# Four graph layers on one core: the first layer's sums on column quarters, TensorE in a written order, and smaller moves at the ends of layers

## The chip, the core and the metric

One core of a Trainium2 chip runs the whole program. The core has TensorE (PE, matrix products into PSUM), VectorE (DVE), ScalarE (ACT), GpSimd (POOL) and SyncE (SP, which issues DMAs here). The metric is the device time of one execution in microseconds (us); the median of several runs is compared.

## The reference, cut to what matters

`x` is 4096 x 256, `adj` 4096 x 4096 (0 or 1). Four attention layers follow each other, each with a residual and a layer norm:

```python
x = _layernorm(x + L0(x, adj, W, a))       # additive attention, 4 heads of 64
x = _layernorm(x + L1(x, adj, Wq, .., bv)) # multi-head attention, 4 heads of 64
x = _layernorm(x + L2(x, adj, W, a))       # additive attention, 1 head
x = _layernorm(x + L3(x, adj, Wq, Wk))     # cosine attention
# L0: e = leaky_relu(s_i[i,h] + s_j[j,h], 0.2), -inf where adj == 0
#     alpha = softmax over j; out = elu(sum_j alpha[i,j,h] * Wh[j,h,:])
# L1: softmax(q k / 8 + (adj.T - 1) * 10000) @ v
# L2: as L0 with one head and slope 0.01
# L3: 0.5 * (softmax(where(adj > 0, Kn @ Qn.T, NEG)) @ x) + 0.5 * x
```

## The kernel before, in words

All matrices are fp32. `X` stays in SBUF: 32 tiles of 128 nodes (`NT`), in 8 blocks of 512 nodes (`NB`, `QB` = 4 tiles a block), with one more column of ones, which gives the softmax denominators in the last layer. Each layer goes over the 8 blocks b of destination nodes, and in each over source tiles j: 32 of 128 rows in layers 0, 2 and 3, and 64 of 64 rows in layer 1. `weights(b, j)` makes the masked, unnormalised attention `prob` of one unit; `sums(b, j)` multiplies it with the values into accumulators in PSUM; when a block is through, outputs are divided, joined with `X` and layer-normed under the next block.

Layer 0 (`additive_heads`): `weights` is four ACT operations (L256, one a head, on a broadcast `row` of the destination's terms) and one DVE multiplication with the mask (L257). `prob` has 8 buffers, `mask` 5 (two units each, loaded by SP). `sums` (L266, L270) runs over a group of four units at a time: first for all units four products with 64 columns of values a head, in column halves of the array, then four with one column of denominators, broadcast to 32 columns, in quarters. `acc` has three PSUM banks, in two buffers, and `ga_ps` two further banks. `prepare(b)` makes the values of four tiles: PE transposes of X (L110), ACT or DVE copies of them (`xT`, L111), products with W (L169), three small ACT exponentials a tile (L171 to L173), and a DVE multiplication into V (L174). `rows(b)` transposes the destination terms (L239), and sends them through DRAM to get `row` on all partitions. `outputs` transposes `kept`, a copy of the finished `acc` (L281), divides, applies elu, and adds to X.

The order on all engines in this layer comes from the framework's scheduler, which follows its own costs and may move one helper's instructions between another's; each engine then runs its list strictly in that order.

Layer 1 (`multi_head_attention`) begins with a prologue: `keys(b)` transposes a block of X, copies it by ACT, and makes keys and queries (L457); `values(b)` makes V (L471). A bound on the scores (`shift`) comes from the largest keys and queries (L490 to L500). The tail of layer 0 (its block 7) stands behind `keys(0)`. In the main part the order of PE, DVE and ACT is written out by hand, three units of lag between `weights` (L526 PE, L528 ACT, L531 DVE) and `sums` (L552). Score tiles `p` have three buffers, which the small PE jobs of `finish` use in turn with them. The row sums of `prob` are collected in three places of `den`: even units by GpSimd (L538), odd units by accumulating DMAs from GpSimd's queue (L544), in two places by turns. `join_sums` (L560) adds these on DVE at j = 7 and 9 of the next block; then follow the row sums on PE (L568), their copy, transpose and reciprocals, and the output in two `half` steps (L584, L587, L592).

Layer 2 (`additive_one`) prepares blocks 0 and 1, then runs layer 1's tail for block 7, then its units. Layer 3 (`cosine_attention`) makes scores (L723), exponentials (L726), masks (L727) and sums (L733), and at a block's end divides, adds 1.5 X, normalises and stores (L744 to L749); the last block in two stores.

Of the kernel before, what the change touches and what calls it, by code (L numbers as in the profile page):

```python
# [9 lines left out]
FP = mybir.dt.float32  # L10
# [4 lines left out]
OP = mybir.AluOpType  # L15
# [3 lines left out]
P = 128  # L19
# [9 lines left out]
def kernel(  # L29
# [47 lines left out]

    X = feat.tile([P, NT, D + 1], FP, name="X")
    nc.vector.memset(X[:, :, D:], 1.0)
# [81 lines left out]
    def additive_values(sb, bank, b, w_sb, V, src, dst, H, slope, busy=False):  # L161

        g = 1.0 - slope
        xT = transposed_block(sb, bank, b, (nc.scalar.copy if busy else nc.vector.tensor_copy, nc.scalar.copy))
        for k in range(QB):
            t = b * QB + k
            pw = bank()
            for c in range(KC):
                nc.tensor.matmul(pw[:, :D + 2 * H], xT[:, c, k * P:(k + 1) * P], w_sb[:, c, :],  # L169
                                 start=(c == 0), stop=(c == KC - 1))  # L170
            nc.scalar.activation(src[:, t, :], pw[:, D:D + H], AF.Exp, scale=g)  # L171
            nc.scalar.activation(dst[:, t, :], pw[:, D + H:D + 2 * H], AF.Exp, scale=g)
            nc.scalar.activation(V[:, t, D:], pw[:, D + H:D + 2 * H], AF.Exp, scale=slope)  # L173
            nc.vector.tensor_tensor(V[:, t, :D].rearrange("p (h d) -> p h d", h=H),  # L174
                                    pw[:, :D].rearrange("p (h d) -> p h d", h=H),
                                    V[:, t, D:].unsqueeze(2).to_broadcast([P, H, D // H]), OP.mult)

    def take(po, rden, H):

        o = fin.tile([P, D], FP, name="o")  # L180
        heads = "p (h d) -> p h d"
        nc.vector.tensor_tensor(o.rearrange(heads, h=H), po.rearrange(heads, h=H),
                                rden.unsqueeze(2).to_broadcast([P, H, D // H]), OP.mult)
        return o
# [11 lines left out]
    def additive_heads(a, H, slope, early, narrow):  # L196
# [7 lines left out]
        with ExitStack() as lay:  # L204
# [13 lines left out]
            mp = pool(lay, "ga_mask", 5)  # L218
# [9 lines left out]
            def first_rows():  # L228
                row[0] = rp.tile([P, H, QW], FP, name="row")
                for h in range(H):  # L230
                    pr = bank()
# [4 lines left out]
            def rows(b):  # L236

                pr = bank()
# [21 lines left out]
            def sums(b, js):  # L260
                if js[0] == 0:
                    acc[b] = pa.tile([P, HC + 1, QW], FP, name="acc")
                for j in js:
                    for h in range(H):
                        lo = (h % 2) * d
                        nc.tensor.matmul(acc[b][lo:lo + d, h // 2, :], V[:, j, h * d:(h + 1) * d], prob[b, j][:, h, :],  # L266
                                         start=(j == 0), stop=(j == NT - 1))
                for j in js:
                    for h in range(H):
                        nc.tensor.matmul(acc[b][h * G:(h + 1) * G, HC, :], V[:, j, D + h:D + h + 1].to_broadcast([P, G]),  # L270
                                         prob[b, j][:, h, :], start=(j == 0), stop=(j == NT - 1))
                if js[-1] == NT - 1:
# [5 lines left out]
            def outputs(bank, b, k):  # L278
                po = bank().rearrange("p (c f) -> p c f", f=P)
                for c in range(HC + 1):  # L280
                    nc.tensor.transpose(po[:, c, :], kept[b][:, c, k * P:(k + 1) * P], ident)  # L281
                rden = fin.tile([P, H], FP, name="rden")
                nc.vector.reciprocal(rden, po[:, HC, ::G])
                add_elu(take(po[:, :HC, :].rearrange("p c f -> p (c f)"), rden, H), b, k, mvs[b])
                if k == QB - 1:
                    layernorm_block(b, mvs[b])
# [571 lines left out]
```

## Time and profile before

| | |
|---|---|
| median of 3 runs | 3020.97 us (3019.48 to 3023.22) |
| profiled execution | 3020.11 us, its span 3018.3 us |
| layer 0, sums | 19.8 to 755.6 us |
| layer 1, prologue | 755.6 to 857.6 us |
| layer 1, main part | 857.6 to about 1793 us |
| layers 2 and 3 | to 3018.3 us |
| PE busy | 2960.5 us |
| granted PE clock | 0.996 of full |

The page of the profile lists busy time by engine; a table by stretches of time gives the same for chosen windows. A timeline line has start, duration, engine, line of the code, operation, tiles, count, and in brackets the idle time ahead of it with what ended it. A line of the waits has the waiting engine, line and tile, what it waited for, and then total us, times, and the longest. Products of fp32 count as two instructions each.

### The profile page before, as it was taken

The page shows a single profiled execution, that of the slowest core. Times are in us where ns is not written, and L with a number is a line of the kernel's source. Part 1 is how long each engine was busy: PE and PEld are TensorE (multiplying, and loading weights), DVE is VectorE, ACT ScalarE, POOL GpSimd, SP SyncE. Part 2 cuts the span into 40 slices and gives each one's busy share as a digit, 9 for nine tenths or more (in the row PEclk, how much of TensorE's full clock was granted, in tenths as well). Part 3 has the DMA queues.
Part 4 walks back from the last instruction along what each step waited for, and adds up shares of the span by engine and source line. Part 5 has one row for each costly group of instructions (what it writes and reads, how often), then busy time and mean ns, then how long its engine had stood idle before and what let it go on. Part 6 is the DMA issues. An engine that isn't in the chain of part 4 may idle for free.

```text
span 3018.3 us, 46664 instructions
## 1 busy us (share of the span) xinstructions
PE 2960.5 (98%) x18557; PEld 1568.0 (52%) x18557; DVE 1972.3 (65%) x2537; ACT 1672.8 (55%) x2653; POOL 862.4 (29%) x598
## 2 busy tenths in 40 slices
PE   9999999999999999999999989999999999999998
PEld 4333333333543333333333338888887777777776
DVE  7799999998457877878778764555655333333333
ACT  6799999997356556566566554444444322222222
POOL 0000000000058888889888860000000000000000
PEclk9999999999999999999999999999999999999999
DMA  7466767665048889889888872444442333333321
GB/s 196 84 134 136 138 133 139 134 121 93 1 108 192 173 179 192 171 183 185 175 183 183 176 173 88 142 154 152 153 140 61 51 56 57 63 50 62 63 49 21
DMA packets 204941, 373.05 MB, mean 124 GB/s; under 512 B 13249, under 2 KB 89009, under 8 KB 203826
## 3 DMA queue, kind: packets, MB, share of 16 engines
q0 software_dynamic: 101120, 176.18, 36.5%
q1 hardware_dynamic: 103328, 193.62, 20.2%
q8 instruction: 145, 2.38, 0.3%
q14 instruction: 74, 0.61, 0.1%
q10 hardware_dynamic: 274, 0.26, 0.0%
HBM read 315.43 MB, written 21.03 MB: 111 GB/s over the span
## 4 chain that ended last, share of the span: by engine, by line
PE 93%; DVE 3%; ACT 2%; issue 1%; DMA 1%; POOL 0%; DVEq 0%; ACTq 0%; POOLq 0%
PE acc L266 15%; PE acc L733 15%; PE p L526 13%; PE acc L552 13%; PE acc L270 8%; PE acc L370 7%; PE g L370 7%; PE p L723 4%; PE g L723 3%; PE g L169 2%; PE g L457 2%; DVE prob L531 1%; ACT p L528 1%; PE g L471 1%; PE acc L684 1%
## 5 line engine op out<-in xcount | busy, mean ns | idle before, releaser
L531 DVE TENSOR_TENSOR prob<-p,mask 128x1024 f32<-128x1024 f32 x512 | 620.4, 1221 | 211.5 <-ACT p L528 200.3
L528 ACT ACTIVATE p<-p,shift 128x1024 f32<-128x1024 f32 x512 | 555.6, 1088 | 347.3 <-PE p L526 337.2
L256 ACT ACTIVATE prob<-row,dst 128x512 f32<-128x512 f32 x1024 | 642.0, 710 | 41.1 <-PE acc L270 38.4
L538 POOL TENSOR_TENSOR den<-den,prob 128x1024 f32<-128x1024 f32 x248 | 615.2, 2481 | 82.1 <-DVE prob L531 72.2
L257 DVE SCALAR_TENSOR_TENSOR prob<-prob,mask 128x2048 f32<-128x2048 f32 x256 | 584.0, 2288 | 45.3 <-ACT prob L256 38.9
L526 PE MATMUL p<-qT,kT 64*64 64x512 f32 x4096 | 531.8, 591 | 10.3 <-DVE prob L531 9.5
L552 PE MATMUL acc<-prob,V 64*64 64x512 f32 x4096 | 531.2, 590 | 8.6 <-DVE prob L531 4.4
L733 PE MATMUL acc<-X,prob 128*128 128x257 f32 x2048 | 486.4, 380 | 2.7 <-DVE prob L727 2.7
L733 PEld LDWEIGHTS acc<-X,prob 128*128 128x128 f32 x2048 | 387.4, 190 | 167.4 <-issue 118.4
L266 PE MATMUL acc<-prob,V 128*64 128x512 f32 x2048 | 461.6, 596 | 0.2 <-DVE prob L257 0.2
L727 DVE TENSOR_TENSOR prob<-prob,mask 128x512 f32<-128x512 f32 x256 | 176.8, 691 | 414.0 <-ACT prob L726 409.5
L721 POOL DMA_DIRECT2D mask<-in_adjT x32 | 28.1, 881 | 1123.2 <-DVE prob L727 562.4
L362 ACT ACTIVATE e<-row,dst 128x512 f32<-128x512 f32 x256 | 184.2, 721 | 239.2 <-DVE prob L364 209.4
L552 PEld LDWEIGHTS acc<-prob,V 64*64 64x64 f32 x4096 | 155.9, 133 | 294.1 <-issue 278.1
L526 PEld LDWEIGHTS p<-qT,kT 64*64 64x64 f32 x4096 | 153.0, 133 | 289.9 <-issue 256.5
L364 DVE SCALAR_TENSOR_TENSOR prob<-e,mask 128x512 f32<-128x512 f32 x256 | 176.3, 689 | 179.5 <-PE acc L370 97.3
L266 PEld LDWEIGHTS acc<-prob,V 128*64 128x64 f32 x2048 | 141.1, 137 | 283.1 <-issue 236.2
L270 PE MATMUL acc<-prob,V 128*32 128x512 f32 x2048 | 237.1, 595 | 0.0
L544 POOL DMA_DIRECT2D den<-prob x240 | 223.0, 929 | 45.0 <-DVE prob L531 39.6
L726 ACT ACTIVATE prob<-p 128x512 f32<-128x512 f32 x144 | 86.0, 597 | 260.2 <-PE p L723 246.2
L370 PE MATMUL g<-V,prob 128*128 128x257 f32 x1024 | 226.5, 380 | 0.0
L370 PE MATMUL acc<-V,prob 128*128 128x257 f32 x1024 | 225.0, 380 | 0.0
(139 smaller groups left out, 2069.8 us busy)
## 6 DMA issues: line engine op xcount, KB each, us to landing
den<-prob POOLq DMA_DIRECT2D x240, 512.0 KB, 5.2
mask<-in_adjT SPq DMA_DIRECT2D x128, 512.0 KB
mask<-in_adjT SPq DMA_DIRECT2D x64, 1024.0 KB
mask<-edges SPq DMA_DIRECT2D x256, 128.0 KB
mask<-in_adjT POOLq DMA_DIRECT2D x32, 1024.0 KB, 8.3
edges<-in_adj POOLq DMA_DIRECT2D x32, 512.0 KB, 9.6
den<-prob SPq DMA_DIRECT2D x16, 512.0 KB
row<-far SPq DMA_DIRECT2D x7, 1024.0 KB
```

Of the source, the lines that this page charges most:

```text
L256: nc.scalar.activation(z[:, h, :], row[b][:, h, :], AF.Relu, bias=-1.0, scale=dst[:, j, h:h + 1])
L257: nc.vector.scalar_tensor_tensor(z, z, 1.0, mask[m][:, j % MJ, :].unsqueeze(1).to_broadcast([P, H, QW]), OP.add, OP.mult)
L266: nc.tensor.matmul(acc[b][lo:lo + d, h // 2, :], V[:, j, h * d:(h + 1) * d], prob[b, j][:, h, :], start=(j == 0), stop=(j == NT - 1))
L270: nc.tensor.matmul(acc[b][h * G:(h + 1) * G, HC, :], V[:, j, D + h:D + h + 1].to_broadcast([P, G]), prob[b, j][:, h, :], start=(j == 0), s ...
L370: nc.tensor.matmul(acc[b][k][:, :D + 1], prob[b, j][:, k * P:(k + 1) * P], V[:, j, :], start=(j == 0), stop=(j == NT - 1))
L526: nc.tensor.matmul(p[c * d:(c + 1) * d, r, :], kT[half, c, j * d:(j + 1) * d], qT[half, c, cols], start=True, stop=True)
L528: nc.scalar.activation(p, p, AF.Exp, bias=shift)
L531: nc.vector.tensor_tensor(z, p, mask[m][:, j % MJ, :].unsqueeze(1).to_broadcast([P, KC, QW]), OP.mult)
L538: nc.gpsimd.tensor_tensor(to, to, flat, OP.add)
L544: nc.gpsimd.dma_start(to, flat, accum_op=OP.add)
L552: nc.tensor.matmul(acc[b][r * d:(r + 1) * d, c, :], V[half, j, r * d:(r + 1) * d], prob[b, j][half, r, :], start=(j == 0), stop=(j == NH - 1))
L733: nc.tensor.matmul(acc[b][k], prob[b, j][:, k * P:(k + 1) * P], X[:, j, :], start=(j == 0), stop=(j == NT - 1))
```

## The change

In layer 0 each unit's sums are twelve products on 32 columns: two for the value columns of each head and one for its denominators; outputs are rearranged to fit. Each unit is summed by itself, two units behind its weights. PE's order there and in the prologue of layer 1 is the order of the program. `prepare` has three tiles in one three-bank accumulator (`side`) and the fourth in a bank, with one set of exponentials and one multiplication for the three. The transposes (`turn`) stand one block ahead of the products. Outputs of a block are transposed two at a time, with the steps of the layer norm at stated units, and the row transpose of the block after next at j = 4. The transposes of block 0 for layer 1 are in the last block of layer 0 (`ahead`). In the prologue of layer 1, `values` of the block before stands between a block's transposes and its keys, and the bound on the scores (`greatest`) between the last two `values`. In the main part the row sums, reciprocals and halves of the block before are at j = 12, 14, 17 and 19 (before: 10, 12, 15 and 18). The two joins of the last block are on GpSimd. In layer 3 the column of X holds twos, 1.5 X is made by ACT eight units ahead of a block's end, and the last two units of the last block are summed accumulator by accumulator. The cut below leaves out removed lines of the first layer's loop, which are in the listing above.

```diff
-    nc.vector.memset(X[:, :, D:], 1.0)
+    nc.vector.memset(X[:, :, D:], 2.0)
...
+    def additive_values(xT, b, groups, w_sb, V, src, dst, H, slope):
         g = 1.0 - slope
-        xT = transposed_block(sb, bank, b, (nc.scalar.copy if busy else nc.vector.tensor_copy, nc.scalar.copy))
-        for k in range(QB):
-            t = b * QB + k
-            pw = bank()
-            for c in range(KC):
-                nc.tensor.matmul(pw[:, :D + 2 * H], xT[:, c, k * P:(k + 1) * P], w_sb[:, c, :],
-                                 start=(c == 0), stop=(c == KC - 1))
-            nc.scalar.activation(src[:, t, :], pw[:, D:D + H], AF.Exp, scale=g)
-            nc.scalar.activation(dst[:, t, :], pw[:, D + H:D + 2 * H], AF.Exp, scale=g)
-            nc.scalar.activation(V[:, t, D:], pw[:, D + H:D + 2 * H], AF.Exp, scale=slope)
-            nc.vector.tensor_tensor(V[:, t, :D].rearrange("p (h d) -> p h d", h=H),
-                                    pw[:, :D].rearrange("p (h d) -> p h d", h=H),
-                                    V[:, t, D:].unsqueeze(2).to_broadcast([P, H, D // H]), OP.mult)
-    def take(po, rden, H):
-        o = fin.tile([P, D], FP, name="o")
-        heads = "p (h d) -> p h d"
-        nc.vector.tensor_tensor(o.rearrange(heads, h=H), po.rearrange(heads, h=H),
-                                rden.unsqueeze(2).to_broadcast([P, H, D // H]), OP.mult)
-        return o
+        heads = "p k (h d) -> p k h d"
+        for k, n, pw in groups:
+            for i in range(n):
+                for c in range(KC):
+                    nc.tensor.matmul(pw[:, i, :D + 2 * H], xT[:, c, (k + i) * P:(k + i + 1) * P], w_sb[:, c, :],
+                                     start=(c == 0), stop=(c == KC - 1))
+            t = slice(b * QB + k, b * QB + k + n)
+            s, d = pw[:, :, D:D + H], pw[:, :, D + H:D + 2 * H]
+            nc.scalar.activation(src[:, t, :], s, AF.Exp, scale=g)
+            nc.scalar.activation(dst[:, t, :], d, AF.Exp, scale=g)
+            nc.scalar.activation(V[:, t, D:], d, AF.Exp, scale=slope)
+            nc.vector.tensor_tensor(V[:, t, :D].rearrange(heads, h=H), pw[:, :, :D].rearrange(heads, h=H),
+                                    V[:, t, D:].unsqueeze(3).to_broadcast([P, n, H, D // H]), OP.mult)
...
-            mp = pool(lay, "ga_mask", 5)
+            mp = pool(lay, "ga_mask", 4)
...
-            def sums(b, js):
-                if js[0] == 0:
+            def sums(b, j):
+                if j == 0:
                     acc[b] = pa.tile([P, HC + 1, QW], FP, name="acc")
-                for j in js:
+                for n in range(HC + 1):
                     for h in range(H):
-                        lo = (h % 2) * d
-                        nc.tensor.matmul(acc[b][lo:lo + d, h // 2, :], V[:, j, h * d:(h + 1) * d], prob[b, j][:, h, :],
+                        lo = h * d + n * G
+                        part = V[:, j, lo:lo + G] if n < HC else V[:, j, D + h:D + h + 1].to_broadcast([P, G])
+                        nc.tensor.matmul(acc[b][h * G:(h + 1) * G, n, :], part, prob[b, j][:, h, :],
                                          start=(j == 0), stop=(j == NT - 1))
-                for j in js:
-                    for h in range(H):
-                        nc.tensor.matmul(acc[b][h * G:(h + 1) * G, HC, :], V[:, j, D + h:D + h + 1].to_broadcast([P, G]),
-                                         prob[b, j][:, h, :], start=(j == 0), stop=(j == NT - 1))
-                if js[-1] == NT - 1:
+                if j == NT - 1:
...
...
+            def turned(bank, b, k):
                 po = bank().rearrange("p (c f) -> p c f", f=P)
                 for c in range(HC + 1):
                     nc.tensor.transpose(po[:, c, :], kept[b][:, c, k * P:(k + 1) * P], ident)
+                return po
+            def outputs(po, b, k):
                 rden = fin.tile([P, H], FP, name="rden")
                 nc.vector.reciprocal(rden, po[:, HC, ::G])
+                o = fin.tile([P, D], FP, name="o")
+                nc.vector.tensor_tensor(o.rearrange("p (h c e) -> p h c e", h=H, c=HC),
+                                        po[:, :HC, :].rearrange("p c (h e) -> p h c e", h=H),
+                                        rden.unsqueeze(2).unsqueeze(3).to_broadcast([P, H, HC, G]), OP.mult)
+                add_elu(o, b, k, mvs[b])
+            def finish(b, j):
+                if j in (4, 10):
+                    k = (j - 4) // 3
+                    pos[b, k], pos[b, k + 1] = turned(bank, b, k), turned(bank, b, k + 1)
+                    if k == 0 and b + 2 < NB:
+                        rows(b + 2, pos[b, 0][:, HC + 1, :])
+                if j in (4, 7, 10, 13):
+                    k = (j - 4) // 3
+                    outputs(pos[b, k], b, k)
+                elif j == 15:
+                    roots[b] = begin_root(mvs[b])
+                elif j == 18:
+                    end_root(*roots[b])
+                elif j in (19, 21, 23, 25):
+                    k = (j - 19) // 2
+                    scale_row(X[:, b * QB + k, :D], mvs[b], roots[b][1], k)
+            def turn(b):
                 if b + 2 < NB:
                     load_x(b + 2)
+                busy = (nc.scalar.copy if b == 0 else nc.vector.tensor_copy, nc.scalar.copy)
+                xTs[b] = transposed_block(sb, bank, b, busy)
+            def prepare(b):
+                groups = [(0, HC + 1, side), (HC + 1, 1, bank().rearrange("p (n f) -> p n f", n=1))]
+                additive_values(xTs[b], b, groups, w_sb, V, src, dst, H, slope)
+            pos, roots, xTs = {}, {}, {}
+            LAG = 2
+            units = [(b, j) for b in range(NB) for j in range(NT)]
+            with tc.manual_schedule(engines={mybir.EngineType.PE}):
+                side = pa.tile([P, HC + 1, QW], FP, name="acc")
+                nc.tensor.matmul(side[:, 0, :], ones[:1, :], a_row, start=True, stop=True)
+                attach(keep, w_sb, side[:, 0, :], H)
+                turn(0)
+                prepare(0)
+                first_rows()
+                turn(1)
+                for i in range(len(units) + LAG):
+                    if i < len(units):
+                        b, j = units[i]
                         weights(b, j)
+                        if (b, j) == (1, 4 * QB):
+                            early()
+                        if i % 8 == 4:
+                            narrow(prob[b, j])
+                    if i >= LAG:
+                        b, j = units[i - LAG]
+                        sums(b, j)
+                        if b:
+                            finish(b - 1, j)
+                    if i == 0 or i % QB == 3 and 3 + i // QB <= NB:
+                        b = 1 if i == 0 else 2 + i // QB
+                        if b + 1 < NB:
+                            turn(b + 1)
+                        prepare(b)
+                        if b == 3:
+                            rows(1, bank())
+                    if i == (NB - 1) * NT + 20:
+                        ahead(bank)
...
+                def turn(b):
+                    xTs[b] = transposed_block(sb, bank, b, (nc.scalar.copy, nc.scalar.copy))
...
-                keys(0)
-                tail(bank)
-                values(0)
-                for b in range(1, NB - 1):
-                    keys(b)
-                    if b < NB - 2:
-                        values(b)
-                keys(NB - 1)
...
+                with tc.manual_schedule(engines={mybir.EngineType.PE}):
+                    keys(0)
+                    tail(bank)
+                    for b in range(1, NB):
+                        turn(b)
+                        if b < NB - 1:
+                            values(b - 1)
+                        keys(b)
+                    values(NB - 2)
+                    greatest()
+                    values(NB - 1)
...
-            def join_sums(b, n):
-                nc.vector.tensor_tensor(den[b][:, 0, :], den[b][:, 0, :], den[b][:, n, :], OP.add)
+            def join_sums(b, n, eng=nc.vector):
+                eng.tensor_tensor(den[b][:, 0, :], den[b][:, 0, :], den[b][:, n, :], OP.add)
...
-                elif j == 10:
+                elif j == 12:
                     row_sums(halves(), b)
-                elif j == 12:
+                elif j == 14:
                     reciprocals(halves(), b)
-                elif j in (15, 18):
-                    half(halves(), b, (j - 15) // 3 * 2)
+                elif j in (17, 19):
+                    half(halves(), b, j - 17)
...
-            join_sums(b, 1)
-            join_sums(b, 2)
+            join_sums(b, 1, nc.gpsimd)
+            join_sums(b, 2, nc.gpsimd)
...
-            def sums(b, j):
-                if j == 0:
+            def sums(b, js):
+                if js[0] == 0:
                     acc[b] = [pa.tile([P, D + 1], FP, name=f"acc{k}") for k in range(QB)]
                 for k in range(QB):
-                    nc.tensor.matmul(acc[b][k], prob[b, j][:, k * P:(k + 1) * P], X[:, j, :],
-                                     start=(j == 0), stop=(j == NT - 1))
+                    for j in js:
+                        nc.tensor.matmul(acc[b][k], prob[b, j][:, k * P:(k + 1) * P], X[:, j, :],
+                                         start=(j == 0), stop=(j == NT - 1))
...
-                        nc.vector.tensor_scalar(y[:, k, :], acc[b][k][:, :D], rden, 0.5, OP.mult, OP.mult)
-                        nc.vector.scalar_tensor_tensor(y[:, k, :], X[:, t, :D], 1.5, y[:, k, :], OP.mult, OP.add)
-                        one_row(mv, k - k0, y[:, k, :])
-                    normalise([y[:, k, :] for k in range(k0, k0 + n)], mv)
-                    nc.sync.dma_start(ov[:, b * QB + k0:b * QB + k0 + n, :], y[:, k0:k0 + n, :])
+                        nc.vector.scalar_tensor_tensor(y[b][:, k, :], acc[b][k][:, :D], rden, y[b][:, k, :], OP.mult, OP.add)
+                        one_row(mv, k - k0, y[b][:, k, :])
...
-                    sums(b, j)
+                    if j == NT - 8:
+                        y[b] = in_.tile([P, QB, D], FP, name="y")
+                        nc.scalar.mul(y[b], X[:, b * QB:(b + 1) * QB, :D], 1.5)
+                    if i < len(units):
+                        sums(b, [j])
+                    elif i > len(units):
+                        sums(b, [j - 1, j])
...
+        def ahead(bank):
+            bm_sb["x"] = transposed_block(wp, bank, 0)
```

## The prediction, made before the change was run

> **What bounds the kernel now.** I read the page first, then the table by stretches of time, TensorE's timeline and the list of waits stage by stage, and last the chain of waits near its end. The page's first line of busy time:
>
> ```profile
> PE 2960.5 (98%) x18557; PEld 1568.0 (52%) x18557; DVE 1972.3 (65%) x2537; ACT 1672.8 (55%) x2653; POOL 862.4 (29%) x598
> ```
>
> TensorE (PE) is busy 98% of 3018.3 us and carries 93% of the chain. Only two things shorten the run: PE doing the same work in less time, and the 58 us in which PE stands still. A busy PE is not PE at its peak, so the timeline of the first layer must say what a matmul costs. One 512-column fp32 product is two instructions. Inside a run, weight loads follow each other every 0.43 us, so an instruction slot is 0.429 us, shared by two products on 64-column tiles and by four on 32-column tiles.
>
> ```profile
> 289.97 7.09 PE L266 MATMUL acc<-prob,V 128*64 128x512 f32 x32
> 296.99 3.64 PE L270 MATMUL acc<-prob,V 128*32 128x512 f32 x32
> 300.56 7.09 PE L266 MATMUL acc<-prob,V 128*64 128x512 f32 x32
> ```
>
> See the starts: 7.02 us for 32 instructions in halves (16 slots = 6.86, so 0.16 over), 3.57 for 32 in quarters (8 slots = 3.43, 0.14 over). About 0.15 us is lost whenever the tile shape changes. In block 0 it is worse, because other work cuts these runs:
>
> ```profile
> 34.47 0.60 PE L110 MATMUL g<-ident,X 128*128 128x128 f32 x4
> 35.00 1.07 PE L266 MATMUL acc<-prob,V 128*64 128x512 f32 x2
> 36.01 1.90 PE L270 MATMUL acc<-prob,V 128*32 128x512 f32 x10
> 37.84 0.66 PE L110 MATMUL g<-ident,X 128*128 128x128 f32 x4
> ```
>
> Here one head alone (x2) takes 1.01 us, although two heads could share those slots. How near the other engines are, from the table by stretches over one later block (us busy):
>
> ```profile
> 256.30:343.12 86.82, 86.82 (x529) 26.48 (x525) 82.28 (x70) 81.77 (x138) 3.85 (x8) 1.00 0.66 134
> ```
>
> The columns are PE, weight loads, VectorE (DVE), ScalarE (ACT), GpSimd. PE has no gap; DVE needs 82.3 and ACT 81.8 of 86.8. That is the floor under any gain of PE here. PE's waits in the first layer sum to some 6 us, most of it at the start. Its waits in the layer-1 prologue, in the main part of layer 1, and at the change to layer 2 are:
>
> ```profile
> PE g L457 <- ACT xT L111: 3.4, 8, 1.5
> PE g L496 <- DVE qtop L491: 1.9, 1, 1.9
> ...
> PE p L526 <- DVE prob L531: 9.5, 15, 1.1
> PE p L568 <- DVE den L560: 8.2, 7, 1.2
> PE acc L552 <- DVE kept L557: 4.3, 7, 0.9
> ...
> PE acc L552 <- DVE prob L531: 4.4, 1, 4.4
> PE g L110 <- DVE kept L557: 4.4, 1, 4.4
> ```
>
> **What the Trainium skill says.** "TensorEngine Tiling (Array Packing)", Key Properties: changing the tiling mode drains the array, and tiles run independently. The trace agrees with both: 0.14 to 0.16 us a change, four 32-column products in one slot. "TensorE: Matmul & The Clock Gate", Architectural detail: ACT and DVE are strict FIFO, and PE only pulls weight loads ahead. The trace shows the FIFO at 1788.83 us, where a join that waits 3.76 us for a DMA holds back a product mask. "SBUF — State Buffer", SBUF: two separate sides: a DVE operation with two SBUF inputs and a GpSimd operation exclude each other. The trace agrees: L592 takes 0.68 us alone and up to 2.44 under a GpSimd addition.
>
> **The change, part by part.**
>
> *First layer, blocks 1 to 7 (148.1 to 755.63, 607.5 us).* A unit is now 12 products on 32 columns instead of 4 on 64 and 4 on 32: 24 instructions, 6 slots, 2.573 us, and no change of shape. Before it was 10.59/4 = 2.647. A block's sums are 32 x 2.573 = 82.3. The output transposes now come in two groups of six: 6 x 0.11 us each (the step from L281 x3, 0.48, to x12, 1.47), 0.15 into and 0.15 out of their shape, plus 0.1 for the row transpose, together 2.0. A block is 84.4 against 86.8, and seven save about 17 us. Transposing block 0 for layer 1 moves into the last block: +1.2. Net 15.5. ACT at 81.8 and DVE at 82.3 fit, with 2 us to spare; eight `prob` buffers give about five units (13 us) of lead, which covers the stretch of j 4 to 25 where DVE has the outputs (22 x 2.2 plus some 11, against 58.6 of PE). SP's `mask` ring goes from 5 tiles to 4: eight units or 20 us ahead is still far over a landing of 10 us, and no wait for `mask` is on the list in this layer; I cost it at 0. The row DMAs are queued about four units later, and masks behind them on SP: 0, at worst 2 us a block. Range of the part: 5 to 17.
>
> *First layer, block 0 (19.8 to 148.1, 128.3 us).* The trace has 97.9 us of sums there (64.7 L266 + 33.2 L270), against 82.3 uncut, and 34.6 of L169 and L110. New, in a fixed order: 82.3, then 96 L169 instructions x 0.223 = 21.4, 40 transposes x 0.11 = 4.4, and 13 changes of shape, 2: 110. The start should be alike: initial values, `first_rows` and two turns put the first sum near 20.5. ACT saves six small activations a group (0.17 each, partly pipelined), and DVE's two multiplications on V cost about 1.4 instead of 4 x 0.42: both hidden, since 4 units need 10.0 + 1.6 of ACT and 8.8 + 2.1 of DVE under 15.4 of PE. New wait: the fourth value group takes the bank of the first transposes, so PE waits for DVE's copy of `xT`. PE has 3.4 us of own work before it, and the copy needs 0.7 plus at most one or two 2.2 us products ahead of it in DVE's FIFO: 0 to 2 us six times, I take 0.5. Behind that wait on PE stand the next sums, then ACT and DVE through the `prob` buffers. Block ends near 133.5: 14.5 us gained, range 7 to 17.
>
> *Layer 1, prologue (755.63 to 857.64).* Block 0's transposes (1.05) and the 1.51 wait behind them leave; five or six waits of 0.24 to 0.29 for `xT` are hidden by `values` of the block before (3.65 us of PE against a copy of 0.6); block 7 keeps its 0.38. The 1.9 us wait for `qtop` goes under `values` of block 6. Sum 5.5, range 2 to 6.5. The 0.8 us wait for V at its end stays.
>
> *Layer 1, main part.* Row sums come two units (3.4 us) later, which removes the 1.17 us wait seven times: 8.2. But the two output halves move from 3 units apart to 2. Each gives DVE 0.68 + 2.44 (locked out by L538) beside 2.4 of products in 3.44 us of PE. Following the three `p` buffers by hand, I get about 1.3 us of PE waits a block, where the trace has 0.48: +0.9 x 7 = 6. Net 2 gained. Not shown before in this spacing, so from 8 gained to 6 lost.
>
> *Change to layer 2.* Two joins of 1.22 us on DVE, which waited 3.76 and 5.56 us for accumulating DMAs, go to GpSimd at 2.48 each (L538). DVE is then free for the last product mask, `kept` and `xT`: both 4.4 us waits of PE go. The new chain is last mask at about 1786.8, DMA out at 1787.6 and landed by 1793.6, or by 1797 if the first join is issued ahead of it, second join done between 1796 and 1800. Its user, the row sums L568, stands behind two preparations of PE, near 1802. Hidden by 2 to 6 us. Half a microsecond may come back from `kept` and `xT` copies meeting. 8.2 gained, range 3 to 9.
>
> *Last layer.* `y` = 1.5 X on ACT (about 1.1 us, under ACT's 2 us of idle time a unit) and the row of twos take one 0.48 us operation out of four in the final DVE chain: 4 x 0.4. The last two units are summed k by k, so the first accumulator is done 1.5 us earlier (4 instructions after the last-but-two unit, in place of 10). The chain from 3007.22 to the last scaling at 3014.15 then ends some 2.8 us earlier, range 1.5 to 3.5. Earlier blocks' outputs have no PE wait: 0.
>
> **Sum.** 15.5 + 14.5 + 5.5 + 2 + 8.2 + 2.8 = 48.5 us. The profiled execution took 3020.11 (span 3018.3 and 1.8 around it), 0.9 below the median of 3020.97: 3020.11 - 48.5 = 2971.6, about 2972. All best ends: 2960; all worst, 18 gained: 3003.
>
> **Rivals.**
> (a) *ACT and DVE become the bound in layer 0.* For: 82 us of 84.4, and PE's fixed order turns each late prob into a wait of PE. Against: five units of lead. If blocks run at 86 us, 11 of the gain go, and with 0.5 us more per preparation and 4 lost in layer 1 it ends near 2990.
> (b) *Slower: quarters don't keep the slot.* If the value products, with three accumulator banks in turn and a fresh weight tile for every product, took a longer slot than L270, 256 units x 6 slots multiply it: 0.03 us a slot is 47 us and eats everything, 0.1 makes it 3077. Against it: L270 already runs on quarters with the same four moving operands at 0.446 us a slot with its change of shape, and its loads of 0.11 us are hidden.
> (c) *The fixed order undoes the whole.* A stall of PE for `xT`, rows or `mask` of 6 us a block in layer 0 gives 48 us back: no change. Against it: everything awaited is issued four units or more ahead.
>
> **Chances.** Forecast as worked out (2960 to 2982) 0.66; (a) 0.23; (b) 0.05; (c) 0.06, half of it past zero. 0.2% of 3021 is 6 us, about what a measurement of this kernel can tell from no change. Faster 0.90, within 0.03, slower 0.07. The range of 8 in 10 is 2960 to 2991: the forecast and most of (a).
>
> **What would show it.** Right: one row of 128*32 sums with starts 2.57 us apart; blocks of 84 to 85 us; layer 0 ending near 727; L568 with no wait; the joins on GpSimd and the first transposes of layer 2 within 2 us of the last L552. Wrong: quarter runs above 0.44 us a slot; PE idle for DVE or ACT in layer 0 over 10 us; waits of L526 up by more than 8 us.

## The result and the profile after

The changed kernel takes 2971.24 us in the median against 3022.09 before: a ratio of 0.983, 95% interval 0.9813 to 0.9848. The forecast was 2972. The profiled execution has a span of 2969.5 us against 3018.3, 48.8 us less. The four runs of the changed kernel lie between 2966.5 us, with a mean granted clock of 0.999, and 2974.6 with 0.997. Each stage below is read from one profiled execution of either kernel, between starts that both timelines show:

| stage, us | before | after | gained | forecast |
|---|---|---|---|---|
| start to the first sum | 19.8 | 24.9 | -5.1 | -0.7 |
| layer 0, block 0 | 128.3 | 110.2 | 18.1 | 15.2 |
| layer 0, blocks 1 to 7 | 607.5 | 591.8 | 15.7 | 15.5 |
| layer 1, prologue, to the first score product | 102.0 | 94.7 | 7.3 | 5.5 |
| layer 1, main part, to the last score product | 925.6 | 921.9 | 3.8 | 2 |
| change to layer 2, to its first run of x18 (L370, now L400) | 40.7 | 33.3 | 7.4 | 8.2 |
| on to the last sums of layer 3 | 1179.1 | 1179.7 | -0.6 | 0 |
| end | 15.2 | 13.1 | 2.1 | 2.8 |

The end of block 0 is where the rows of block 1 begin in the trace of before (148.1), and is counted back from the first output transposes, five units after it, in the trace of after (147.89 - 5 x 2.57 = 135.0).

The page's line of busy time of the changed kernel; PE's idle time falls from 57.8 us to 43.6, so the larger part of the gain is work that PE does in less time:

```profile
PE 2925.9 (99%) x20605; PEld 1567.0 (53%) x20605; DVE 1961.3 (66%) x2488; ACT 1672.6 (56%) x2612; POOL 895.7 (30%) x600
```

TensorE's timeline of block 0. The sums are one row L259 on 32 columns, now cut only once in four units, between two whole preparations:

```profile
49.86 10.51 PE L259 MATMUL acc<-prob,V 128*32 128x512 f32 x96
60.30 1.09 PE L111 MATMUL g<-ident,X 128*128 128x128 f32 x8
61.23 2.84 PE L169 MATMUL acc<-w_sb,xT 128*128 128x264 f32 x12
63.90 1.05 PE L169 MATMUL g<-w_sb,xT 128*128 128x264 f32 x4
```

The row of 96 lasts 10.44 us to the next start: 24 slots of 0.429 are 10.29, and 0.15 the one change of shape. The table by stretches, over one later block (PE, weight loads, DVE, ACT, GpSimd; clock, DMA share, GB/s):

```profile
165.10:249.50 84.40, 84.40 (x783) 26.09 (x781) 81.35 (x71) 81.07 (x138) 5.90 (x8) 1.00 0.64 137
```

PE is still without a gap, at the 84.4 us that were worked out, with 3 us between it and DVE. TensorE's waits over the whole run, those of layer 1 and of the change to layer 2:

```profile
PE p L561 <- DVE prob L566: 14.4, 15, 1.5
...
PE g L603 <- POOL den L595: 2.6, 1, 2.6
...
PE g L111 <- DVE kept L592: 0.8, 1, 0.8
```

The wait for the joins ahead of the row sums (8.2) is gone, the wait of score products for masks has grown from 9.5 to 14.4, and at the change two waits of 4.4 us have become 0.8 and a new one of 2.6, for the GpSimd join.

The waits are not all of the gain at that change. The granted clock, the column behind the busy times in the table by stretches, isn't full there. The stage of before, that of the changed kernel, and the same code again in the run with the output halves apart (below), which changes nothing in this stage:

```profile
1783.27:1824.00 40.73, 31.57 (x171) 21.95 (x163) 20.46 (x45) 13.35 (x54) 4.96 (x4) 0.83 0.50 143
1743.41:1776.76 33.35, 29.46 (x171) 21.01 (x163) 18.21 (x43) 13.36 (x54) 9.54 (x6) 0.95 0.62 174
1737.71:1769.25 31.54, 27.77 (x170) 19.65 (x163) 18.19 (x43) 13.35 (x54) 9.53 (x6) 1.00 0.66 184
```

In the trace of before the clock is at half for 13.65 us of this stage, from 1790.71 on, and in that of the changed kernel for 3.41 us; in the third there is no such stretch. So PE's idle time fell by 5.3 us (9.2 to 3.9), and the same products took 2.1 us less. The third line shows that a further 1.7 us depend on the clock alone, since its code here and its wait for the join (2.5 us) are those of the changed kernel. The clock drops while or just after PE waits in the traces that show it, but waits of 2.5 to 2.8 us with no drop are in three runs (output halves apart, and both with value products in the two banks); what decides is open.

### The profile page after: what moved, and what is told of

Its sections match the earlier page's. It is cut to its first block, busy times and chain, and to the rows that moved or that the text cites. A ratio compares the mean times of both kernels' runs of the same rounds, so it can differ in the third digit from the quotient of the medians.

```text
span 2969.5 us, 50734 instructions
## 1 busy us (share of the span) xinstructions
PE 2925.9 (99%) x20605; PEld 1567.0 (53%) x20605; DVE 1961.3 (66%) x2488; ACT 1672.6 (56%) x2612; POOL 895.7 (30%) x600
## 4 chain that ended last, share of the span: by engine, by line
PE 95%; DVE 2%; ACT 1%; DMA 1%; issue 0%; POOL 0%; DVEq 0%; POOLq 0%; ACTq 0%
PE acc L259 22%; PE acc L769 15%; PE p L561 14%; PE acc L587 13%; PE acc L400 8%; PE g L400 7%; PE p L758 4%; PE g L758 3%; PE g L489 2%; DVE prob L566 1%; PE g L503 1%; PE g L169 1%; ACT p L563 1%; PE acc L169 1%; PE acc L719 1%; PE g L111 1%
## 5 line engine op out<-in xcount | busy, mean ns | idle before, releaser
L259 PE MATMUL acc<-prob,V 128*32 128x512 f32 x6144 | 663.8, 592 | 0.0
L573 POOL TENSOR_TENSOR den<-den,prob 128x1024 f32<-128x1024 f32 x248 | 626.9, 2528 | 65.7 <-DVE prob L566 55.2
L248 ACT ACTIVATE prob<-row,dst 128x512 f32<-128x512 f32 x1024 | 635.6, 710 | 1.7 <-DVE row L227 1.7
L561 PE MATMUL p<-qT,kT 64*64 64x512 f32 x4096 | 532.1, 591 | 15.2 <-DVE prob L566 14.4
L259 PEld LDWEIGHTS acc<-prob,V 128*32 128x32 f32 x6144 | 197.4, 110 | 451.6 <-issue 433.2
L579 POOL DMA_DIRECT2D den<-prob x240 | 231.0, 962 | 52.8 <-DVE prob L566 47.9
L818 POOL COPY tick<-prob 128x1 f32<-128x1 f32 x32 | 34.9, 1091 | 651.6 <-DVE prob L249 651.6
L400 PE MATMUL g<-V,prob 128*128 128x257 f32 x1024 | 226.5, 380 | 0.0
L400 PE MATMUL acc<-V,prob 128*128 128x257 f32 x1024 | 225.8, 381 | 0.0
```

Of the source, the lines that this page charges most:

```text
L248: nc.scalar.activation(z[:, h, :], row[b][:, h, :], AF.Relu, bias=-1.0, scale=dst[:, j, h:h + 1])
L259: nc.tensor.matmul(acc[b][h * G:(h + 1) * G, n, :], part, prob[b, j][:, h, :], start=(j == 0), stop=(j == NT - 1))
L400: nc.tensor.matmul(acc[b][k][:, :D + 1], prob[b, j][:, k * P:(k + 1) * P], V[:, j, :], start=(j == 0), stop=(j == NT - 1))
L561: nc.tensor.matmul(p[c * d:(c + 1) * d, r, :], kT[half, c, j * d:(j + 1) * d], qT[half, c, cols], start=True, stop=True)
L573: nc.gpsimd.tensor_tensor(to, to, flat, OP.add)
L579: nc.gpsimd.dma_start(to, flat, accum_op=OP.add)
```

## The experiments

Ten kernels were run. My theory: in layer 0 changes of tile shape and cuts of the rows of sums were the cost; elsewhere, waits of a FIFO (an engine's list, which it runs strictly in order). The rivals stand in each expectation. "Stage" means a row of the table above. The kernel before and the changed kernel measured 3021 to 3023 and 2971 us.

**Halves again, in each unit** (on the changed kernel; the output is taken in the old arrangement):

```diff
-                for n in range(HC + 1):
-                    for h in range(H):   # 12 products on 32 columns
+                for h in range(H):       # 4 on 64 columns
+                    lo = (h % 2) * d
+                    nc.tensor.matmul(acc[b][lo:lo + d, h // 2, :], V[:, j, h * d:(h + 1) * d], ..)
+                for h in range(H):       # 4 on 32 columns
+                    nc.tensor.matmul(acc[b][h * G:(h + 1) * G, HC, :], ..)
```

> The changed kernel with one thing undone: in layer 0 a unit is again four products on 64 columns and four on 32, but unit by unit, in the same written order. Theory (the gain of the quarters is the shape changes that they avoid, 0.15 us each): every unit now has two changes, 256 x 0.30 = 77 us more, blocks of 84.4 + 9.6 = 94 us, about 3048 us in all. Rival (slots on quarters are simply faster, or the order of the program is all that counts, and a change of shape is free inside a fixed order): unit 2.57 to 2.65 us, 2971 to 2990.

Measured: 3042.5 us, 1.0069 (1.0054 to 1.0084) of before. Layer 0 from first sum to first keys takes 772.6 us against 702.0. The timeline of this kernel, where only starts matter:

```profile
300.23 1.94 PE L257 MATMUL acc<-prob,V 128*64 128x512 f32 x8
302.10 1.06 PE L260 MATMUL acc<-prob,V 128*32 128x512 f32 x8
303.10 1.94 PE L257 MATMUL acc<-prob,V 128*64 128x512 f32 x8
```

A unit is 2.86 us in the mean of a block against 2.575: the same six slots and two changes of shape of 0.14. So a change of shape costs close to 0.15 us under a fixed order too; the rival falls. 70.6 us were added, where 77 were expected: 256 units with two changes are 73.5 us, not 77, and each of the 21 pieces of other work between the rows of sums stands in for one of the changes.

**Quarters alone, on the kernel before:**

```diff
                 for j in js:
-                    for h in range(H): ...   # halves, then denominators in quarters
+                    for n in range(HC + 1):
+                        for h in range(H): ...   # 12 products on 32 columns
```

> The kernel before with the quarters alone: its groups of four units, its scheduler's order and everything else stay, only the products of layer 0 are twelve on 32 columns and the output is rearranged. Theory: in blocks 1 to 7 the 0.30 us of each of 8 groups go, 2.4 us a block, 17 us; in block 0 the change inside each group and the lone heads go, though other work still cuts the runs, 5 to 10 us. About 2997 us. Rival (the written order carries the gain of layer 0): under 8 us gained, 3013 or more.

Measured: 3003.4 us, 0.9942 (0.9927 to 0.9956): 18.0 us gained, where 24 were expected; of them 16.7 in layer 0's sums, half of that stage's 33.8. A block is 85.2 us (row transposes at 228.68 and 313.89): 1.6 less, where 2.4 were expected, since the four outputs and the row transpose of a block stood at changes of shape before, and now cut a row that has none. Block 0 falls by 5.3 us, to 123.0. The rival of a written order that carries all is refuted from this side. The rest of the stage belongs to the other edits: 0.8 us in each later block, which has two cuts in place of five, and 12.8 in block 0, less 1.2 for the transposes that came in.

**TensorE's order in layer 0 left to the scheduler** (on the changed kernel):

```diff
-            with tc.manual_schedule(engines={mybir.EngineType.PE}):
+            with ExitStack():
                 side = pa.tile([P, HC + 1, QW], FP, name="acc")
```

> The changed kernel with the order of TensorE in layer 0 left to the scheduler (prologue of layer 1 as changed). Theory: with quarters a cut costs only 0.3 us and no lone head, so the scheduler's order in block 0 costs 3 to 10 us through more cuts and waits for banks, nothing in blocks 1 to 7: 2974 to 2981. Rival (the order is what gained block 0's 13 us): 2984 or more. Second rival (the fixed order cost something): faster than 2971.

Measured: 2968.2 us, 0.9824 (0.9809 to 0.9838). My theory was wrong here: it is no slower. Whether it is faster, as the second rival had it, the whole time doesn't tell, as the intervals overlap. From the first sum on, layer 0 takes 701.9 us against 702.0; and the first sum comes at 20.44 us in place of 24.86. TensorE's waits of the changed kernel over layer 0, and then of this one over its first 140 us, where the wait for the first DMA is the same:

```profile
PE acc L317 <- DMA a_row<-in_a: 2.2, 1, 2.2
PE acc L169 <- ACT xT L112: 1.0, 1, 1.0
PE acc L226 <- DVE row L227: 0.8, 1, 0.8
PE acc L226 <- ACT row L227: 0.7, 1, 0.7
PE acc L226 <- DVE V L176: 0.5, 1, 0.5
PE g L111 <- ACT xT L112: 0.5, 1, 0.5
PE g L111 <- ACT row L227: 0.2, 1, 0.2
```

```profile
PE g L169 <- issue: 0.4, 1, 0.4
PE acc L226 <- DVE V L176: 0.4, 1, 0.4
```

The written order pays 3.7 us of waits after the first DMA against 0.8 here, in the chain from X to the first row, where there is nothing else that may come first; the scheduler puts the transposes of blocks 1 and 2 and the values of block 1 into these gaps. Not all of the 4.4 us is order, though. In each trace the records of the clock begin with a step to full, and the products ahead of it run at half the pace of later ones. The step comes at 12.95 us in the changed kernel and at 8.63 here. The first products of the changed kernel, to be set beside the 2.84 us of the same row above:

```profile
7.45 5.62 PE L169 MATMUL acc<-w_sb,xT 128*128 128x264 f32 x12 [1.00 <-ACT xT L112]
```

Runs with steps at like times part the two: at 10.5 and 11.0 us the written order has its first sum at 23.8 and 24.1 (halves in each unit; last joins on DVE), and at 10.6 and 11.0 the scheduler's has it at 21.7 and 21.6 (three edits; value products in banks, below). The order costs about 2.3 us there, and the rest of the 4.4 goes with the step. The order is thus no source of the gain in layer 0.

**Then what made block 0 shorter? Banks.** Two kernels with the value products tile by tile in the two banks, the three-bank `side` not used by the preparations: one in the written order, one in the scheduler's:

```diff
-                groups = [(0, HC + 1, side), (HC + 1, 1, bank()..)]
+                groups = ((k, 1, bank()..) for k in range(QB))
```

> The changed kernel with the value products of layer 0 tile by tile in the two banks (four sets of exponentials and multiplications a block, as before), in the written order. Theory (block 0 gained because three tiles fit in one PSUM tile, so that TensorE runs a whole preparation without waiting for its evacuation): the third and fourth tile of a preparation wait for DVE's multiplication, which stands behind products of 2.2 us in its FIFO: 1 to 3 us twice, in seven preparations 14 to 40 us of new waits for V, 2985 to 3010. Rival (banks don't matter, the written order does): block 0 still 110 us, 2971.

> The same, with TensorE's order in layer 0 left to the scheduler. Theory: it puts sums between the value products again, as before the change, and pays with changes of shape: few waits, but block 0 118 to 123 us in place of 110, about 2976 to 2980. Rival (the scheduler does as well with banks): block 0 within 2 us of 110, about 2968.

Measured: 2985.4 us (0.9875, 0.9846 to 0.9904) and 2978.9 (0.9853, 0.9825 to 0.9882). Block 0 takes 122.2 and 122.5 us in place of 110.2. The two pay in different coin. TensorE's waits of the first over its first 140 us, and the timeline of the second:

```profile
PE g L169 <- DVE V L176: 5.3, 8, 1.6
```

```profile
47.76 1.05 PE L259 MATMUL acc<-prob,V 128*32 128x512 f32 x4
48.74 2.05 PE L169 MATMUL g<-w_sb,xT 128*128 128x264 f32 x8
50.72 1.06 PE L259 MATMUL acc<-prob,V 128*32 128x512 f32 x6
```

In the written order PE stands and waits for V and `xT` (less than I expected: the waits of L169 sum to 7.7 us, 6.2 of them in block 0, not 14 to 40), and 3.41 us at half the clock (38.88 to 42.29) cost another 1.7; the remaining 4 us of block 0 are not itemised here. In the scheduler's order PE fills the time with scraps of sums, each between two changes of shape. So the group of three tiles is worth 10 to 12 us in either order. It does two things, which these runs don't part: it gives a preparation room in PSUM, and it needs two sets of exponentials and multiplications where the banks need four.

**The last joins back on DVE:**

```diff
-            join_sums(b, 1, nc.gpsimd)
-            join_sums(b, 2, nc.gpsimd)
+            join_sums(b, 1)
+            join_sums(b, 2)
```

> The changed kernel with the two last joins of layer 1 back on DVE. Theory (the joins wait for DMAs at the head of DVE's queue and hold back the last mask, kept and xT): the two waits of TensorE of 4.4 us come back and the wait of 2.6 us for the GpSimd join goes; from the last score product to the first products of layer 2's block 0 in a run it takes 41 us in place of 33.5: 6 to 7.5 us more, about 2978. Rival (the gain there came from the other order of preparations, not from the joins): within 2 us of 2971.

Measured: 2979.9 us, 0.9863 (0.9847 to 0.988). The stage takes 41.3 us against 33.3. The timeline of DVE and PE in this kernel shows the mechanism, a join in the FIFO ahead of the last mask and of `kept`:

```profile
1749.04 1.23 DVE L595 TENSOR_TENSOR den<-den 128x1024 f32<-128x1024 f32 x1 [3.64 <-DMA den<-prob]
1750.18 1.22 DVE L566 TENSOR_TENSOR prob<-p,mask 128x1024 f32<-128x1024 f32 x1
1751.45 1.68 PE L587 MATMUL acc<-prob,V 64*64 64x512 f32 x8 [4.24 <-DVE prob L566]
1757.41 1.23 DVE L595 TENSOR_TENSOR den<-den 128x1024 f32<-128x1024 f32 x1 [6.01 <-DMA den<-prob]
```

PE is idle for 9.8 us of the stage, as before the change (9.2), and the clock is at half for 13.65 us again (from 1751.82): PE's products take 31.5 us against 29.5. So of the 7.9 us, 5.9 are idle time and 2.0 pace.

**The last DMA ahead of the first join** (on the changed kernel). In its timeline the first join stands ahead of the last accumulating DMA, and three mask loads of layer 2 on SP's queue as well:

```profile
1748.07 1.48 SPq L390 DMA_DIRECT2D mask<-in_adjT  x3
1748.91 2.35 POOL L595 TENSOR_TENSOR den<-den 128x1024 f32<-128x1024 f32 x1 [1.18 <-DMA den<-prob]
1751.20 0.87 POOL L579 DMA_DIRECT2D den<-prob  x1
1760.49 2.33 POOL L595 TENSOR_TENSOR den<-den 128x1024 f32<-128x1024 f32 x1 [8.42 <-DMA den<-prob]
```

```diff
+            with tc.issue_after(last):      # the DMA into den of j = 63
-            join_sums(b, 1, nc.gpsimd)
+                join_sums(b, 1, nc.gpsimd)
             join_sums(b, 2, nc.gpsimd)
```

> The changed kernel with the first of the two last joins held behind the issue of the last accumulating DMA on GpSimd's queue (after: the join stands ahead of it, and the DMA is issued 3.1 us after the masks of layer 2 on SP and lands 9.2 us later). Theory (the DMA is late, first by the join ahead of it, then by three 1 MB mask loads that it queues behind): issued near 3.5 us earlier, it lands after 5 to 6 us, the second join ends some 5 us earlier, and TensorE's wait of 2.6 us for it goes: about 2968.5. Rival (the masks slow the DMA anyway, since they come 0.4 us behind it): it lands 8 to 9 us after its issue, the wait shrinks by the 3.5 us of the earlier issue all the same. Second rival (the first accumulators of layer 2 wait for something else right after): the wait goes and the products of layer 2 start no earlier.

Measured: 2968.0 us, 0.9819 (0.9802 to 0.9835), within the interval of the changed kernel, so the stage must tell: 29.8 us against 33.3. This kernel's timeline of GpSimd:

```profile
1749.34 0.87 POOL L579 DMA_DIRECT2D den<-prob  x1
...
1756.82 2.37 POOL L595 TENSOR_TENSOR den<-den 128x1024 f32<-128x1024 f32 x1 [3.90 <-DMA den<-prob]
```

The DMA lands 7.5 us after its issue, between theory and rival, and PE's wait is gone. Half of the 3.6 us is not the edit's: the clock stays full here, and three runs without the edit in which it did so too have this stage at 31.5 to 31.9 us. Against these the edit gains 1.8 to 2.1 us. The time from the DMA's issue to the join that waits for it goes with the masks' place: 5.3 us in the kernel before (masks 1.8 us behind it), 7.5 here (0.4 behind), 9.3 in the changed kernel (3.1 ahead). The other runs fall in line: 5.3 and 5.7 us with masks 1.8 and 1.5 behind, 7.6 at 0.4 behind, 8.9 to 9.6 at 3.1 to 3.5 ahead. That the masks are the reason is argued from this order; they were not moved by themselves.

**The second output half one unit later:**

```diff
-                elif j in (17, 19):
-                    half(halves(), b, j - 17)
+                elif j in (17, 20):
+                    half(halves(), b, (j - 17) // 3 * 2)
```

> The changed kernel with the second output half of a block in layer 1 at j = 20 in place of 19, three units after the first. Theory (two halves within two units put two locked 2.4 us additions close together on DVE, and TensorE waits 1.1 to 1.5 us for a score mask): that wait falls to the 0.48 us of before, seven times 0.7 to 1.0: waits of the score products from 13.6 to about 8 us, main part 5 us shorter, about 2966. Rival (the wait comes from the locked addition itself, wherever the second half stands, since an even unit's GpSimd addition now starts beside it): no shorter, within 1.5 us.

Measured: 2965.3 us, 0.9809 (0.9795 to 0.9824). The main part of layer 1 takes 916.5 us against 921.9. Its waits of the score products over the whole run, of this kernel:

```profile
PE p L561 <- DVE prob L566: 9.2, 15, 1.0
```

It was 14.4 us in the changed kernel. So the place of the second half did cost 5 us. What of it did is open, since the edit changed two things: the spacing, and how much of a GpSimd addition (on even units) DVE's addition to X meets. The second half's addition in one block, in the changed kernel and then in this one:

```profile
976.46 2.43 DVE L627 TENSOR_TENSOR X<-X,oh 128x512 f32<-128x512 f32 x1
977.25 1.30 DVE L627 TENSOR_TENSOR X<-X,oh 128x512 f32<-128x512 f32 x1
```

In both cases it ends 0.55 us after GpSimd's addition (at 978.34 and 978.00), but in this kernel it begins later within that. It takes 2.43 us or more in all seven blocks of the changed kernel, and 1.30 in six and 1.90 in one here, as in the kernel before (1.30 to 1.32). So the rival's forecast, no shorter wherever the half stands, failed; but that DVE's addition held back by GpSimd's makes the wait is not refuted, as that addition itself became shorter.

**The prologue of layer 1 in its earlier sequence** (PE's order there is left to the scheduler again as well):

```diff
-                    for b in range(1, NB):
-                        turn(b)
-                        if b < NB - 1:
-                            values(b - 1)
-                        keys(b)
-                    values(NB - 2)
-                    greatest()
+                    # turn(b), keys(b), values(b) for each b; greatest() ahead of the last two values
```

> The changed kernel with the prologue of layer 1 in its earlier sequence and order (transposes directly ahead of their keys, the bound on the scores ahead of the last values, order left to the scheduler); block 0's transposes stay in layer 0. Theory (the gain there is waits for copies): six waits of 0.24 to 0.29 us and the 1.9 us for the bound come back, and 0.1 us a block in which transposes drain: from the first keys to the first scores 94.7 + 4 = 98.7 us, about 2975. Rival (most of the 7.3 us came from the transposes that moved to layer 0): within 1.5 us of 2971.

Measured: 2975.5 us, 0.9845 (0.983 to 0.9859), which overlaps the changed kernel; the stage shows it: 100.2 us against 94.7. Waits for `xT` are 1.9 in place of 0.4, and the 1.9 for `qtop` is back. The last `values` take 8.8 us in one row where two rows took 7.4 and a wait of 0.8 for V followed: 3.41 us at half the clock begin there (818.27), behind the wait for `qtop`, so some 0.6 us of the 5.5 are pace. Sequence and written order were undone together; which of them gains is not shown.

**Three edits together**, the free order in layer 0, the half at j = 20, the DMA first:

> Three edits on the changed kernel at once, each in a stage of its own: TensorE's order in layer 0 left to the scheduler, the second output half of layer 1 at j = 20, and the first last join behind the last accumulating DMA. Theory: 3.8 us from the start, 5 from layer 1, 2.6 from the change to layer 2: 11 us, about 2960. Rival for the second and third as said for them alone: 2964 to 2967.

Measured: 2959.0 us, 0.9789 (0.9775 to 0.9804), clear of the changed kernel's 0.9813 to 0.9848 and the fastest of all. First sum at 21.7 us (24.9), main part 916.5 (921.9), change to layer 2 30.2 (33.3): 3.1 + 5.4 + 3.1 = 11.6, of 12.1 in the span. The single gains add up. Some 1 us of the start (the clock's step is at 10.63 us, not 12.95) and 1.8 of the change (no stretch at half the clock) are differences of the clock, which runs without these edits show too.

## Why the prediction was right, and where not

*Blocks 1 to 7: right in mechanism and size.* 15.7 us against 15.5, block 84.40 against 84.4. The slot of 0.429 us, read from quarters that stood there already, held for three times as many, so rival (b), longer slots, was wrong; and PE kept its lead over ACT and DVE, so (a) was too.

*Block 0: right sum, wrong split.* 110.2 us against 110, but with no wait in place of the 3 us that I put in, and the first sum 4.4 us later than forecast. The step that failed is "the start should be alike": I costed the operations of the start, but neither that the written order leaves PE no other work while ACT and DVE copy (3.7 us of waits), nor the clock, whose step to full came at 8.95 us before and at 12.95 after. In the scheduler's order with the step at 8.63 the first sum is at 20.44, the 20.5 of the forecast. I also gave the fixed order a part in block 0's gain; the free order did as well. Of the 18.1 us, 5.3 came with the quarters alone, and 10 to 12 with the group of three.

*Prologue: 7.3 against 5.5.* The term of waits was right; it left out that the seams became cheaper too (0.96 us from transposes to the next row in place of 1.09 plus the wait); why is not shown.

*Main part of layer 1: 3.8 against 2.* The 8.2 us of row sums went, and the added wait of the halves was forecast as 6 and is 4.9 by the lists (1.14 and 1.50 us in two blocks looked at, 1.3 forecast). The 3.8 is a lucky reading: eight runs of this main part lie between 921.9 and 923.7 us, two of the earlier one at 924.9 and 925.6, so 1 to 4 us were gained.

*Change to layer 2: 7.4 against 8.2, in part by luck.* Both 4.4 us waits shrank as said. "Hidden by 2 to 6 us" failed: the forecast lets the last DMA land 6 us after its issue, and it took 9.3, so PE waited 2.6 us and its idle time fell by 5.3 alone. The other 2.1 us are products that ran at half the clock before, a term that the forecast put at nothing.

*Last layer: 2.1 against 2.8.* The sum took the final DVE chain as bound by DVE alone. After the change it runs at PE's pace: the third and fourth reciprocals stand 0.89 us apart, as four instructions of 0.217 do, and only what follows the last accumulator is shorter by the operation removed. Here the profile is of the changed kernel:

```profile
2960.97 0.17 DVE L778 RECIPROCAL rden<-acc 128x1 f32<-128x1 f32 x1
...
2961.86 0.15 DVE L778 RECIPROCAL rden<-acc 128x1 f32<-128x1 f32 x1
```

The total came out nearer than its terms, and that is luck: +2.9, +1.8 and +1.8 us against -4.4, -0.8, -0.6 and -0.7. Two sums beside it are wrong by their own numbers, though no conclusion rests on them: the worst ends of the parts add up to 12.5 us gained, not 18, and 0.1 us more on 256 x 6 slots is 154 us, so some 3126, not 3077.

## What to carry to other kernels

Read slot and seam apart: starts inside a run give the price of the work, and starts across it the price of a change of shape, and count the seams. A preparation that cannot run whole costs either waits or scraps; try a wider tile with fewer operations behind it before an order written by hand, which gained nothing in layer 0. Before a small difference of a stage is put down to an edit, set the granted clock of that stage beside it, and look for a run with the same code there. An operation that waits for a DMA doesn't belong in the FIFO of an engine that others wait for, and the DMA it waits for belongs ahead of it and, as far as these runs tell, ahead of bulk loads.

## What the runs showed of the hardware that I had not expected

The same accumulating DMA of 512 KB took 5.3, 7.5 or 9.3 us to the start of the join behind it, with three 1 MB loads 1.8 us behind it, 0.4 behind, or 3.1 ahead. The clock is not full for a whole run: in the trace of before it is at half for 13.65 us at the change to layer 2, where PE waited twice for 4.4 us, and three runs with one wait of 2.5 to 2.8 us there show no drop. And the first products of a run are slow and vary with it: twelve value products take 5.41 us to the next start in the changed kernel, with the clock's step to full at 12.95 us, 4.13 in the kernel with halves, with the step at 10.54, and 2.67 later on. The table by stretches reads 1.00 ahead of that step because no record of the clock lies there; that it was at half is inferred from the pace.
